# Expert biases as columns, an identity transposed at the head, indices in three operations, and a new plan for a two-layer kernel

## The chip, the cores and the metric

The kernel runs on one core of a Trainium2 chip. Its engines are TensorE (PE, matmuls), VectorE (DVE), ScalarE (ACT), GpSimd (POOL) and SyncE (SP, which here only issues transfers). The metric is the device time in microseconds (us) of one execution, as a median of several. A profiled execution gives a trace of every instruction; its times are counted from the start of its span.

## What is computed

Eight sequences (B = 8) of 512 positions and 256 features pass through two layers. The first is a feed-forward layer whose weights are chosen for each sequence from eight experts by an index. The second is an attention layer with 16 heads of 16 features, with a bias for every head and pair of positions and a mask, scaled and shifted by an embedding of a timestep, and a feed-forward layer behind it. Everything is fp32.

```python
h = gelu(x @ Wi[e] + bi[e]); o = h @ Wo[e] + bo[e]          # e = expert index of the sequence
x = layernorm(o + x) * gamma[e] + beta[e]
emb = silu(sin_emb(timestep)) @ W_ada + b_ada
x = layernorm(x) * (1 + scale) + shift                       # scale, shift from emb
q, k, v = x @ Wq + bq, x @ Wk + bk, x @ Wv + bv              # 16 heads
p = softmax(where(mask, -inf, q @ k.T / 4 + fside))
x = x + (p @ v) @ Wo + bo
x = x + gelu2(layernorm(x) * g2 + beta2) @ W1 ... @ W2 + b2  # 1024 hidden features
```

An index that is negative counts from the end and is then held within 0 to 7, as array indexing does.

## The kernel before

**A planner orders the work.** The kernel doesn't write its instructions in the order of its loops. Each piece of work is an operation (`op`) with an engine, a cost, a key, operations that it depends on, and buffers that it takes and uses. `Weave.run` then simulates the engines: at each turn it takes, for every engine, the operations that could start earliest, picks among those within 0.25 us the one of the lowest key (with an extra charge for another activation table or another way of tiling PE), and emits the one that starts first. Only operations with a key up to 14 above the lowest unfinished one are considered. The order of the program on each engine is that order; at run time the engines are held together by semaphores alone. The keys are in units of score steps.

**The work.** For every sequence b there are these groups:
- *Up*: 8 tiles of hidden features, each two accumulating 128x512 matmuls (`up`, line 687), and a Gelu on ScalarE (line 792) whose per-partition bias is a column of the tile `bc[b]`. Up needs the transposed input `xt` and the weights `wi[b]`.
- *Down*: 4 tiles of rows, each 8 accumulating 128x256 matmuls (line 710), and on VectorE an addition (line 805) and row statistics.
- *Norm*: two layer norms on GpSimd, ScalarE and VectorE.
- *Project* (line 861; transposes at line 665) and *values* (line 909): queries, keys and values.
- 16 *score steps*, of 32 query rows each for all heads, 128 in all. A step loads 1 MB of `fside` (line 1108), forms scores in four PSUM banks (lines 1138 and 1145), adds the bias and takes the row maximum on VectorE (line 1168), takes the exponential on ScalarE (line 1189) and transposes 32x32 blocks on VectorE (line 1204). In odd steps GpSimd adds the mask (line 1160). After every fourth step PE sums the values (line 1244) and multiplies by the output weights (line 1287).
- *last norm, last up, last down*: the second feed-forward layer, for the last sequence in three parts (line 1050). Its two hidden matmul groups use lines 687 and 710 as well.

An fp32 matmul is two pairs of a weight load and a matmul in the trace. All matmuls but the score and value sums use one of four PSUM buffers, `d`.

**The places.** `place` spreads the operations of a group evenly, by cost, from the first number of its entry in `PLACES` to the second; the third is how much lower the keys of its VectorE, ScalarE and GpSimd operations are. `DUE` and `LAST_DUE` give the keys of a step's operations relative to the step, `AHEAD` how far ahead of its first user a weight load is keyed, `PUT_BACK` the extra charges.

**The head.** The eight expert indices are loaded by a ScalarE DMA, turned into numbers within 0 to 7 by five VectorE operations on one row of eight (lines 391 to 397), and read by SyncE (line 431). Only then can SyncE issue the loads of the first expert's weights, the first `wi` in four pieces (line 474). GpSimd builds a 128x128 identity, `ident`.

**The expert bias** of 1024 numbers is loaded as 8 rows of 128 (line 462, `br`), transposed by PE against the identity (line 777), and copied to `bc` by VectorE (line 781). Another small transpose of this kind, for the shared biases, is at line 565.

**Instruction packets.** PE's instructions come from memory in packets of 256, by DMA. The planner counts PE's instructions (`words`), and takes it that the next packet is asked for at word 155 of each 256, and needed at word 192; it lands 2.4 us after it is seen by a queue. PE operations that would run past the last packet on hand are delayed in the plan. A load of 0.3 MB or more isn't started in the plan until `CLEAR` microseconds after a packet was asked for, and at run time such a load waits for the PE operation that ends behind that point (`behind`).

Of the kernel before, what the change touches and what calls it, by code (L numbers as in the profile page):

```python
# [16 lines left out]
ALU = mybir.AluOpType  # L17
AX = mybir.AxisListType

P = 128  # L20
# [10 lines left out]
def _constants():  # L31
# [13 lines left out]
    for i in range(TURN_PIECES):  # L45
# [14 lines left out]
        (-38.45, -36.16, 8.44), (-17.59, -11.52, -8.19), (7.71, 9.93, 7.56), (16.68, 26.05, 3.41),  # L60
        (37.04, 39.22, 1.41), (59.52, 58.14, 7.23), (76.02, 83.59, 6.09), (97.99, 99.88, 6.32),
    ],
    "down": [
        (-14.3, -13.78, 4.95), (-7.57, 12.25, 5.14), (10.35, 8.93, 1.84), (18.31, 19.88, 3.05),
        (44.73, 48.47, 6.47), (60.22, 65.93, -5.3), (73.23, 78.37, -3.77), (99.19, 102.84, 4.19),
    ],
    "norm": [
        (9.12, -14.45, 12.84), (42.79, 181.18, 28.12), (35.59, 134.32, 11.46),
        (2.52, 203.96, -36.01), (60.29, 31.67, 7.3), (7.93, 107.02, -50.91), (98.6, -8.09, 1.62),
        (119.85, -6.52, 12.88),  # L70
    ],
    "project": [
        (-12.18, -6.14, -12.38), (15.67, 19.49, 12.1), (24.45, 26.05, -2.29),
        (42.28, 58.66, 8.57), (55.4, 64.48, -4.5), (77, 88.71, 1.56), (87.84, 91.44, -7.27),
        (100.45, 117.32, -1.06),
    ],
    "values": [
        (3.18, -1.06, 7.82), (14.22, 38.5, 0.11), (40.15, 46.1, 4.42), (52.04, 62.66, 4.96),
        (64.28, 58.7, -11.65), (93.83, 89.56, 8.58), (110.2, 99.31, 6), (116.12, 120, 0.53),
    ],  # L80
    "last_norm": [
        (20.41, 6.88, -6.37), (35.57, 32.95, -7.85), (65.08, 42.97, -1.38), (80.61, 90.62, 2.89),
        (95.86, 82.62, 2.14), (101.58, 123.81, 3.25), (118.43, 130.96, -4.04),
    ],
    "last_up": [
        (28.71, 24.51, 4.43), (37.76, 39, -1.21), (60.99, 61.58, -1.11), (80.88, 87.68, 3.16),
        (102.11, 103.74, -0.13), (112.29, 122.71, -5.66), (126.48, 119.28, -4.58),
    ],
    "last_down": [
        (32.43, 20.21, -5.44), (59.59, 50.14, 4.98), (69.93, 70.07, 2.47), (87.34, 92.75, -0.01),  # L90
        (110.17, 115.86, 6.8), (124.14, 122.32, 5.45), (137.59, 134.49, -0.85),
    ],
    "last_part": [
        (131.42, 236.07, 2.43), (198.84, 229.52, -5.61), (222.05, 209.79, -2.84),
# [4 lines left out]
    "load_m": 2.79, "load_f": 2.99, "convert": 5.91, "add": 4.01, "neg": -0.08, "exp": 6.61,  # L99
    "turn": 9.37, "rec": 12.83, "diagonal": 7.66, "sums0": 5.09, "sums1": 6.11, "sums2": 12.85,  # L100
    "sums3": 7.94, "own": 7.57, "spread": 7.08, "divide": 7.96, "out": 9.83, "out_add": 12.81,
    "load_f2": 3.09, "masked": -0.48,
}
LAST_DUE = {
    "exp": 3.04, "turn": 11.23, "neg": 7.38, "rec": 14.33, "diagonal": 11, "sums0": 22.52,
    "sums1": 14.89, "sums2": 27.57, "sums3": 50.95, "own": 37.8, "spread": 42.01, "divide": 72.21,
    "out": 66.26, "out_add": 80.74,
# [3 lines left out]
    "table": 11.03, "tiles": 0.92,  # L111
# [3 lines left out]
    "xt": 6.18, "wi": 1.31, "br": 5.1, "x": 4.75, "wo": -1.82, "row": 23.23, "w1": -3.09,  # L115
    "w2": -0.62, "ss": 5.17, "bo": 18.56,
# [25 lines left out]
class Weave:  # L142
# [11 lines left out]
    CLEAR = 1.5  # L154

    def __init__(self):
        self.ops = []
# [21 lines left out]
    def run(self, behind):  # L179
# [11 lines left out]
        count, needed, asked, lands_at = 0.0, self.NEEDED, self.ASKED, [0.0]  # L191
        queue, clear, gate = 0.0, -100.0, None
        while left:
# [56 lines left out]
            if o.words:  # L250
                if count + o.words > needed:
                    needed += self.PACKET
                    lands_at.pop(0)
                if count + o.words > asked:
                    at = start + (asked - count) / o.words * o.cost
                    lands_at.append(max(at + self.SEEN, queue) + self.TAKES)
                    asked += self.PACKET
                    clear, gate = at + self.CLEAR, None
                count += o.words
# [25 lines left out]
def tile_expert_ffn_then_conditioned_layer(  # L285
# [46 lines left out]
    NJ = S // QB  # L332
    QS = 1.0 / math.sqrt(HD)
# [9 lines left out]
    def const(shape, name, dtype=F32):  # L343
        return pool.tile(shape, dtype, name=name)

    def slots(n, shape, name, dtype=F32):
        return Slots([pool.tile(shape, dtype, name=f"{name}_{i}") for i in range(n)])
# [16 lines left out]
    s_br = slots(2, [NF, P], "br")  # L364
# [26 lines left out]
    nc.vector.tensor_copy(idx_f, idx_in)  # L391
    idx_n = const([1, B], "idx_n")
    nc.vector.tensor_scalar(idx_n, idx_f, 0.0, float(E), ALU.is_lt, ALU.mult)
    nc.vector.tensor_tensor(idx_f, idx_f, idx_n, ALU.add)
    nc.vector.tensor_scalar(idx_f, idx_f, 0.0, float(E - 1), ALU.max, ALU.min)
    idx = const([1, B], "idx", I32)
    nc.vector.tensor_copy(idx, idx_f)
# [14 lines left out]

    def load(mb, key, emit, **kw):
        return op("SP", w.ISSUE, key, emit, mb=mb, **kw)

    xn, xt_h = [s_xn.new() for _ in range(B)], [s_xt.new() for _ in range(B)]
    br, bc = ([s.new() for _ in range(B)] for s in (s_br, s_bc))
# [11 lines left out]
    def at_expert(b):  # L429
        if b not in index:  # L430
            index[b] = nc.sync.value_load(idx[0:1, b : b + 1], min_val=0, max_val=E - 1)
        return bass.ds(index[b], 1)
# [8 lines left out]
    def load_first(b, mb, key, what, emit, **kw):  # L441
        return load_ahead(mb, what, emit, **kw) if b else load(mb, key, emit, **kw)

    ld_x, ld_xt, ld_wi, ld_wo, ld_bo_e, ld_rows, ld_br = {}, {}, {}, {}, {}, {}, {}
    for b in range(B):
# [15 lines left out]
        def br_in(b=b):  # L461
            nc.sync.dma_start(br[b].tile, e_bi[at_expert(b)].rearrange("o (c p) -> (o c) p", p=P))
# [20 lines left out]
        ld_br[b] = load_first(b, 0.02, -38.97, "br", br_in, takes=[br[b]])  # L483
# [286 lines left out]
    def expert_layer(b):  # L770
# [3 lines left out]
        h = s_d.new()  # L774
        a = op(
            "PE", 0.2, 0,
            lambda: nc.tensor.transpose(h.tile[:, :NF], br[b].tile, ident[:NF, :NF]),
            deps=[ld_br[b]], takes=[h], uses=[br[b]], words=2,
        )
        e = op(  # L780
            "DVE", 0.2, 0, lambda: nc.vector.tensor_copy(bc[b].tile, h.tile[:, :NF]),
            deps=[a], takes=[bc[b]], uses=[h],
        )
        turned = (0.2, [(a, 0.0), (e, -1.0)])
# [4 lines left out]
        def make(f, h, a):  # L789
            return op(  # L790
                "ACT", 0.7, 0,
                lambda: nc.scalar.activation(  # L792
                    hid.tile[:, f, :], h.tile, AF.Gelu, bias=bc[b].tile[:, f : f + 1]
                ),
                deps=[a, e], uses=[h, bc[b], hid], table="gelu",
            )

        hids = up(first, lambda: rising(wi[b]), (ld_wi[b], wi[b]), xt, [ld_xt[b]], hid, make)
        first.insert(3 if b == 0 else 0, turned)
# [295 lines left out]
    def attention_step(s):  # L1095
# [61 lines left out]
        if not joins:  # L1157
            for u in range(NU):
                def put_mask(u=u):
                    nc.gpsimd.tensor_tensor(f()[:, u, :], f()[:, u, :], mh.tile, ALU.add)  # L1160

                masked[u] = op(
                    "POOL", 1.25, s + due("masked", s), put_mask, deps=[lf, mc], uses=[pair, mh]
                )
# [182 lines left out]
def _laid_out(name, a):  # L1347
# [10 lines left out]
    elif name == "x":  # L1358
        b, s, d = a.shape
        a = a.reshape(b, s // P, P, d).transpose(0, 2, 1, 3)  # L1360
    elif name == "L0_cond_Wo":
# [48 lines left out]
```

## Time and profile before

| | |
|---|---|
| median of 3 runs | 908.43 us (904.48 to 909.48) |
| profiled execution | 906.64 us |
| its span, first to last instruction | 904.8 us |
| 128x512 matmuls of line 687 | 480 |
| 128x256 matmuls of line 710 | 1024 |
| score matmuls, line 1145 | 2048 |
| value sums, line 1244 | 8192 |
| first and last score step | at 73.3 and 858.5 us |
| bytes moved by DMA | 198.00 MB, 219 GB/s |
| GpSimd busy, ScalarE busy | 603.6 us, 687.1 us |

A row of the timeline gives the start, how long the row lasts, the engine (PEld is PE loading weights; a q behind a name is its queue), the line, the operation, the tile written and those read, the shape, how many instructions the row merges, and in brackets the idle time of the engine before it and what ended that. A row of the waits gives the engine, its line, what it waited for, and then microseconds in total, the number of waits, and the longest. "issue" is a wait for nothing that the profile shows, the arrival of instructions among it. The durations of matmuls include their way through the array, so they overlap; the spacing of their starts says how fast they follow each other.

### The profile page before, as it was taken

How to read it: one execution, taken by the hardware profiler on the slowest of the kernel's cores; microseconds unless marked ns; L12 is line 12 of the kernel's file. 1: busy time of each engine (PE TensorE's matmuls, PEld its weight loads, DVE VectorE, ACT ScalarE, POOL GpSimd, SP SyncE). 2: the span in 40 equal slices, each digit the busy share in tenths (PEclk: the TensorE clock that was granted, in tenths of full speed). 3: DMA queues.
4: the chain of work that ended last, by engine and by line, in shares of the span. 5: the costliest groups of instructions: out<-in, count | busy, mean ns of one | idle time of the engine just before them, and what ended most of it. 6: DMA issues, size and time to landing. Idle time of an engine off the chain costs nothing.

```text
span 904.8 us, 32061 instructions
## 1 busy us (share of the span) xinstructions
PE 884.0 (98%) x13329; PEld 522.7 (58%) x13329; DVE 737.5 (82%) x1715; ACT 687.1 (76%) x1522; POOL 603.6 (67%) x716
## 2 busy tenths in 40 slices
PE   7999999999989999999999999999999999999998
PEld 2664464654654655545657557466555555465687
DVE  1227999999978997999978999889789999999841
ACT  2347969869948977699784895998778977988743
POOL 1176887777779746767684976549786876685510
PEclk9999999999999999999999999999999999999999
DMA  6476555555575564666737667536745566665410
GB/s 237 165 299 267 224 215 230 214 204 227 214 313 217 200 245 168 221 254 241 280 136 276 235 245 293 211 133 265 288 163 219 205 242 241 248 242 221 172 60 24
DMA packets 43160, 198.00 MB, mean 219 GB/s; under 512 B 4772, under 2 KB 12278, under 8 KB 24582
## 3 DMA queue, kind: packets, MB, share of 16 engines
q1 hardware_dynamic: 42724, 195.91, 56.9%
q8 instruction: 104, 1.70, 0.8%
q14 instruction: 42, 0.34, 0.1%
q10 hardware_dynamic: 290, 0.04, 0.0%
HBM read 191.73 MB, written 4.21 MB: 217 GB/s over the span
## 4 chain that ended last, share of the span: by engine, by line
PE 87%; DMA 5%; ACT 3%; issue 2%; POOL 1%; DVE 1%; SPq 1%; DVEq 0%; POOLq 0%; ACTq 0%
PE d L710 23%; PE d L687 20%; PE d L1244 13%; PE sc L1145 12%; PE d L861 6%; DMA fs<-in_fside_Bx16xSxS_dram 3%; PE d L1287 3%; PE d L909 3%; PE sc L1138 2%; PE d L665 2%; PE d L1050 2%; ACT fs L1189 1%; POOL fs L1160 1%; PE d L1260 1%; DMA wo_t<-in_L_cond_Wo_dram 1%
## 5 line engine op out<-in xcount | busy, mean ns | idle before, releaser
L1189 ACT ACTIVATE fs<-fs,top 128x512 f32<-128x512 f32 x512 | 363.1, 712 | 62.1 <-POOL top L1181 61.6
L1168 DVE CUSTOM_DVE_ANT_0 fs<-sc,fs 128x512 f32<-128x512 f32 x512 | 325.2, 683 | 41.2 <-PE sc L1145 18.7
L1160 POOL TENSOR_TENSOR fs<-fs,mh 128x512 f32<-128x512 f32 x256 | 291.0, 1163 | 44.3 <-DMA fs<-in_fside_Bx16xSxS_dram 36.3
L1204 DVE STREAM_TRANSPOSE fs<-fs 128x1024 f32<-128x1024 f32 x256 | 304.9, 1219 | 4.9 <-ACT fs L1189 4.7
L710 PE MATMUL d<-w,hid 128*128 128x256 f32 x1024 | 239.7, 385 | 0.0
L687 PE MATMUL d<-xt,w 128*128 128x512 f32 x480 | 224.2, 607 | 8.1 <-DMA w<-in_L_cond_Wi_dram 6.7
L710 PEld LDWEIGHTS d<-w,hid 128*128 128x128 f32 x1024 | 189.1, 190 | 59.0 <-issue 31.1
L687 PEld LDWEIGHTS d<-xt,w 128*128 128x128 f32 x480 | 87.2, 191 | 123.2 <-issue 97.1
L1244 PEld LDWEIGHTS d<-fs,vb 64*32 64x32 f32 x8192 | 113.3, 105 | 48.1 <-issue 34.0
L1145 PE MATMUL sc<-k,q 32*64 32x512 f32 x2048 | 139.2, 600 | 0.0
L1244 PE MATMUL d<-fs,vb 64*32 64x128 f32 x8192 | 133.2, 272 | 2.4 <-issue 2.4
L1189 ACT ACTIVATION_READ_ACCUMULATOR fs<-fs,top 128x1 f32 x512 | 96.9, 189 | 0.0
L1120 POOL TENSOR_SCALAR mh<-m 128x512 bf16<-128x512 uint8 x128 | 79.7, 622 | 25.0 <-PE sc L1138 9.3
L1181 POOL TENSOR_SCALAR top<-top 128x4 f32<-128x4 f32 x128 | 25.4, 198 | 104.1 <-DVE top L1168 98.0
L792 ACT ACTIVATE hid<-d,bc 128x512 f32<-128x512 f32 x64 | 41.4, 686 | 29.1 <-PE d L687 19.9
L1145 PEld LDWEIGHTS sc<-k,q 32*64 32x64 f32 x2048 | 36.2, 130 | 32.9 <-issue 14.6
L728 DVE BATCH_NORM_STATS2 st<-xn 128x6 f32<-128x256 f32 x96 | 40.2, 419 | 15.5 <-POOL xn L762 13.3
L1189 ACT ACT_TABLE_LOAD x36 | 46.2, 1283 | 0.6
L1225 POOL TENSOR_TENSOR dg<-cst,den 128x512 f32<-128x512 f32 x32 | 34.1, 1066 | 17.1 <-DVE den L1220 14.5
L1168 DVE DVE_READ_ACCUMULATOR2_ANT top<- 128x1 f32 x512 | 42.5, 83 | 0.0
L984 ACT ACTIVATE hid<-d,col 128x512 f32<-128x512 f32 x56 | 35.9, 686 | 7.5 <-PE d L687 7.2
L762 POOL TENSOR_TENSOR xn<-xn,rows 128x1024 f32<-128x1024 f32 x16 | 37.9, 2371 | 4.8 <-ACT xn L741 4.0
(100 smaller groups left out, 753.3 us busy)
## 6 DMA issues: line engine op xcount, KB each, us to landing
fs<-in_fside_Bx16xSxS_dram SPq DMA_DIRECT2D x128, 1024.0 KB, 8.1
w<-in_L_cond_W_dram SPq DMA_DIRECT2D x16, 1024.0 KB, 6.4
w<-in_L_cond_Wo_dram SPq DMA_DIRECT2D x8, 1024.0 KB, 10.6
m<-in_mask_Bx1xSxS_bk_dram SPq DMA_DIRECT2D x32, 256.0 KB, 5.4
w<-in_L_cond_Wi_dram SPq DMA_DIRECT2D x7, 1024.0 KB, 6.0
xt<-in_x_turned_dram SPq DMA_DIRECT2D x8, 512.0 KB, 3.7
xn<-in_x_dram SPq DMA_DIRECT2D x8, 512.0 KB
out_dram<-xn SPq DMA_DIRECT2D x32, 128.0 KB, 3.4
```

The lines of the kernel that those rows point to most:

```text
L687: nc.tensor.matmul(h.tile, wt[:, c, f * P : (f + 1) * P], src.tile[:, c, :], start=(c == 0), stop=(c == ND - 1),)
L710: nc.tensor.matmul(h.tile[:, :D], lhs(f), wt[:, f, :], start=(f == 0), stop=(f == n - 1))
L728: nc.vector.bn_stats(st, src[:, t, :])
L792: lambda: nc.scalar.activation(hid.tile[:, f, :], h.tile, AF.Gelu, bias=bc[b].tile[:, f : f + 1]),
L861: nc.tensor.matmul(h.tile, wt[:, c, g * P : (g + 1) * P], x1t.tile[:, c, :], start=(c == 0), stop=(c == ND - 1),)
L1120: nc.gpsimd.tensor_scalar(mh.tile, m8.tile[:, s % NI, :].bitcast(U8), MASKED, 1.0, ALU.mult, ALU.mult)
L1145: nc.tensor.matmul(banks[u][64 * r : 64 * r + 64, :], q_h[b].tile[quads[u], r, i, :], k_h[b].tile[quads[u], r, :], start=not joins, stop=True,
L1160: nc.gpsimd.tensor_tensor(f()[:, u, :], f()[:, u, :], mh.tile, ALU.add)
L1168: nc.vector.tensor_tensor_reduce(out=f()[:, u, :], in0=banks[u], in1=f()[:, u, :], scale=1.0, scalar=-3.0e38, op0=ALU.add, op1=ALU.max, ac ...
L1189: nc.scalar.activation(f()[:, u, :], f()[:, u, :], AF.Exp, bias=top.tile[:, u : u + 1], accum_out=den.tile[:, u, s % NI : s % NI + 1],)
L1204: nc.vector.transpose(two, two)
L1244: nc.tensor.matmul(pc[r].tile[QB * u : QB * u + QB, :P], vb_h[b].tile[half, j, u, :], t[half, :, :, u, QB * j : QB * j + QB], start=(j == ...
```

## The change

- Indices: the cast to f32 is left out, the comparison and the addition read the int32 row, and the last operation writes int32. Three VectorE operations in place of five.
- Head: 18 transposes of the identity are issued on PE ahead of everything else, into a PSUM buffer that is not read. They need only `ident`. The planner's count of PE's instructions starts at 36.
- Expert biases: the input is laid out by the host as (expert, 128, 8), so that a DMA writes `bc[b]` directly, 8 numbers to each of 128 partitions. The transposes at line 777 and the copies at line 781 go, and the Gelus depend on the load itself.
- Planner: a packet is asked for no earlier than the one before it has landed, and `CLEAR` is 0.4 in place of 1.5. The cost of the mask addition is 1.17 in place of 1.25.
- All of `PLACES`, `DUE`, `LAST_DUE`, `PUT_BACK` and `AHEAD` have new numbers.

```diff
--- before.py
+++ after.py
@@ -57,63 +57,64 @@
 
 PLACES = {
     "up": [
-        (-38.45, -36.16, 8.44), (-17.59, -11.52, -8.19), (7.71, 9.93, 7.56), (16.68, 26.05, 3.41),
-        (37.04, 39.22, 1.41), (59.52, 58.14, 7.23), (76.02, 83.59, 6.09), (97.99, 99.88, 6.32),
+        (-35.52, -11.64, 4.94), (-11.9, -22.54, -2.99), (10.31, 12.14, 8.37),
+        (14.25, 22.85, -1.17), (36.77, 36.76, 1.07), (60, 57.83, 3.43), (73.83, 70.58, 4.85),
+        (94.92, 94.18, 8.26),
     ],
     "down": [
-        (-14.3, -13.78, 4.95), (-7.57, 12.25, 5.14), (10.35, 8.93, 1.84), (18.31, 19.88, 3.05),
-        (44.73, 48.47, 6.47), (60.22, 65.93, -5.3), (73.23, 78.37, -3.77), (99.19, 102.84, 4.19),
+        (-27.61, -24.87, -12.02), (-10.68, 13.31, -0.1), (15.13, 9.61, 0.32),
+        (18.1, 22.84, -6.64), (37.6, 44.8, 6.55), (61.84, 71.13, 6.87), (71.01, 75.76, -11.57),
+        (94.27, 108.04, 4.72),
     ],
     "norm": [
-        (9.12, -14.45, 12.84), (42.79, 181.18, 28.12), (35.59, 134.32, 11.46),
-        (2.52, 203.96, -36.01), (60.29, 31.67, 7.3), (7.93, 107.02, -50.91), (98.6, -8.09, 1.62),
-        (119.85, -6.52, 12.88),
+        (16.76, 0.43, 33.63), (50.75, 236.12, 35.78), (19.13, 112.89, 1.36),
+        (-0.73, 150.66, -35.12), (51.98, -3.26, 10.27), (19.84, 116.2, -46.57),
+        (91.19, 25.08, -4.73), (110.17, -11.25, 3.62),
     ],
     "project": [
-        (-12.18, -6.14, -12.38), (15.67, 19.49, 12.1), (24.45, 26.05, -2.29),
-        (42.28, 58.66, 8.57), (55.4, 64.48, -4.5), (77, 88.71, 1.56), (87.84, 91.44, -7.27),
-        (100.45, 117.32, -1.06),
+        (-3.93, 2.03, -2.64), (13.32, 15.26, 2.77), (19.23, 30.34, -1.82), (36.97, 59.93, 8.33),
+        (59.15, 43.96, -0.28), (76.77, 86.46, -0.67), (94.5, 91.24, 3.27), (102.9, 113.31, 0.58),
     ],
     "values": [
-        (3.18, -1.06, 7.82), (14.22, 38.5, 0.11), (40.15, 46.1, 4.42), (52.04, 62.66, 4.96),
-        (64.28, 58.7, -11.65), (93.83, 89.56, 8.58), (110.2, 99.31, 6), (116.12, 120, 0.53),
+        (7.77, 10.24, 3.39), (15.24, 37.1, -8.26), (43.61, 43.86, 7.08), (45.49, 67.83, -2.21),
+        (67.46, 56.65, -3.66), (87.64, 97.81, 9.29), (105.15, 97.2, 1.98), (117.06, 118.69, 4.47),
     ],
     "last_norm": [
-        (20.41, 6.88, -6.37), (35.57, 32.95, -7.85), (65.08, 42.97, -1.38), (80.61, 90.62, 2.89),
-        (95.86, 82.62, 2.14), (101.58, 123.81, 3.25), (118.43, 130.96, -4.04),
+        (18.93, 10.43, -5.55), (50.08, 53.52, 3.27), (67.69, 61.42, 9.62), (72.79, 86.37, -9.45),
+        (92.08, 89.98, -0.52), (115.23, 113.98, 8.28), (117.57, 113.58, -3.53),
     ],
     "last_up": [
-        (28.71, 24.51, 4.43), (37.76, 39, -1.21), (60.99, 61.58, -1.11), (80.88, 87.68, 3.16),
-        (102.11, 103.74, -0.13), (112.29, 122.71, -5.66), (126.48, 119.28, -4.58),
+        (26.27, 38.03, 1.01), (46.54, 47.77, 0.5), (64.51, 62.2, 1.22), (85.68, 84.44, 5.39),
+        (107.94, 99.87, -3.13), (108.88, 120.89, 3.43), (128.3, 135.79, 3.82),
     ],
     "last_down": [
-        (32.43, 20.21, -5.44), (59.59, 50.14, 4.98), (69.93, 70.07, 2.47), (87.34, 92.75, -0.01),
-        (110.17, 115.86, 6.8), (124.14, 122.32, 5.45), (137.59, 134.49, -0.85),
+        (35.14, 24.23, -5.08), (61.9, 51.71, 11.65), (77.75, 75.33, -0.48), (91.52, 78.58, 2.9),
+        (102.76, 117.32, 4.72), (116.43, 125.64, -1.72), (134.83, 134.55, 3.99),
     ],
     "last_part": [
-        (131.42, 236.07, 2.43), (198.84, 229.52, -5.61), (222.05, 209.79, -2.84),
+        (132.72, 239.72, 0.26), (186.35, 240.12, 6.14), (193.91, 245.56, -3.6),
     ],
 }
 
 DUE = {
-    "load_m": 2.79, "load_f": 2.99, "convert": 5.91, "add": 4.01, "neg": -0.08, "exp": 6.61,
-    "turn": 9.37, "rec": 12.83, "diagonal": 7.66, "sums0": 5.09, "sums1": 6.11, "sums2": 12.85,
-    "sums3": 7.94, "own": 7.57, "spread": 7.08, "divide": 7.96, "out": 9.83, "out_add": 12.81,
-    "load_f2": 3.09, "masked": -0.48,
+    "load_m": -10.02, "load_f": -1.89, "convert": 7.1, "add": 3.28, "neg": -0.39, "exp": 5.75,
+    "turn": 9.93, "rec": 13.65, "diagonal": 9.39, "sums0": 8.89, "sums1": 5.6, "sums2": 10.17,
+    "sums3": 6.54, "own": 5.17, "spread": 6.3, "divide": 6, "out": 5.97, "out_add": 12.92,
+    "load_f2": -1.22, "masked": 0.86,
 }
 LAST_DUE = {
-    "exp": 3.04, "turn": 11.23, "neg": 7.38, "rec": 14.33, "diagonal": 11, "sums0": 22.52,
-    "sums1": 14.89, "sums2": 27.57, "sums3": 50.95, "own": 37.8, "spread": 42.01, "divide": 72.21,
-    "out": 66.26, "out_add": 80.74,
+    "exp": 5.76, "turn": 8.18, "neg": 13.36, "rec": 10.03, "diagonal": 19.1, "sums0": 23.45,
+    "sums1": 25.82, "sums2": 41.29, "sums3": 33.28, "own": 38.66, "spread": 31.04,
+    "divide": 34.93, "out": 67.43, "out_add": 77.99,
 }
 
 PUT_BACK = {
-    "table": 11.03, "tiles": 0.92,
+    "table": 7.19, "tiles": 0.72,
 }
 
 AHEAD = {
-    "xt": 6.18, "wi": 1.31, "br": 5.1, "x": 4.75, "wo": -1.82, "row": 23.23, "w1": -3.09,
-    "w2": -0.62, "ss": 5.17, "bo": 18.56,
+    "xt": 1.02, "wi": 3.02, "br": 19.67, "x": -1.86, "wo": 2.29, "row": 24.21, "w1": 7.1,
+    "w2": 8.89, "ss": -2.85, "bo": 20.55,
 }
 
 
@@ -151,10 +152,10 @@
     CHANGE = {"dense": 0.2, "scores": 0.1, "sums": 0.14}
     PACKET, ASKED, NEEDED, SEEN, TAKES = 256.0, 155.0, 192.0, 1.0, 2.4
     ISSUE, BEGINS, RATE, LANDS, LARGE, NEAR, HOLD = 0.45, 1.2, 0.37, 0.8, 0.3, 100.0, 4.0
-    CLEAR = 1.5
+    CLEAR = 0.4
 
     def __init__(self):
-        self.ops = []
+        self.ops, self.sent = [], 0.0
 
     def op(self, engine, cost, key, emit, deps=(), takes=(), uses=(), table=None, mb=0.0,
            words=0, tiles="dense"):
@@ -188,8 +189,8 @@
                 open_ops[o.engine].append(o)
         by_key = sorted(self.ops, key=lambda o: o.key)
         lowest, table, tiles, left = 0, None, None, len(self.ops)
-        count, needed, asked, lands_at = 0.0, self.NEEDED, self.ASKED, [0.0]
-        queue, clear, gate = 0.0, -100.0, None
+        count, needed, asked, lands_at = self.sent, self.NEEDED, self.ASKED, [0.0]
+        queue, clear, gate, landed = 0.0, -100.0, None, 0.0
         while left:
             while by_key[lowest].done:
                 lowest += 1
@@ -252,8 +253,9 @@
                     needed += self.PACKET
                     lands_at.pop(0)
                 if count + o.words > asked:
-                    at = start + (asked - count) / o.words * o.cost
-                    lands_at.append(max(at + self.SEEN, queue) + self.TAKES)
+                    at = max(start + (asked - count) / o.words * o.cost, landed)
+                    landed = max(at + self.SEEN, queue) + self.TAKES
+                    lands_at.append(landed)
                     asked += self.PACKET
                     clear, gate = at + self.CLEAR, None
                 count += o.words
@@ -330,6 +332,7 @@
     NU = 4
     NI = P // QB
     NJ = S // QB
+    WARM = 18
     QS = 1.0 / math.sqrt(HD)
 
     pool = ctx.enter_context(tc.tile_pool(name="sb", bufs=1))
@@ -361,7 +364,6 @@
     s_w = slots(2, [P, NF * D], "w")
     s_bo = slots(2, [P, D], "bo")
     s_rows = slots(2, [P, 2, D], "rows")
-    s_br = slots(2, [NF, P], "br")
     s_bc = slots(2, [P, NF], "bc")
     s_xt = slots(2, [P, ND, S], "xt")
     s_q = slots(2, [P, ND, NQ, 2 * QB], "q")
@@ -388,13 +390,10 @@
     ident = const([P, P], "ident")
     make_identity(nc, ident)
     idx_f = const([1, B], "idx_f")
-    nc.vector.tensor_copy(idx_f, idx_in)
-    idx_n = const([1, B], "idx_n")
-    nc.vector.tensor_scalar(idx_n, idx_f, 0.0, float(E), ALU.is_lt, ALU.mult)
-    nc.vector.tensor_tensor(idx_f, idx_f, idx_n, ALU.add)
-    nc.vector.tensor_scalar(idx_f, idx_f, 0.0, float(E - 1), ALU.max, ALU.min)
+    nc.vector.tensor_scalar(idx_f, idx_in, 0.0, float(E), ALU.is_lt, ALU.mult)
+    nc.vector.tensor_tensor(idx_f, idx_in, idx_f, ALU.add)
     idx = const([1, B], "idx", I32)
-    nc.vector.tensor_copy(idx, idx_f)
+    nc.vector.tensor_scalar(idx, idx_f, 0.0, float(E - 1), ALU.max, ALU.min)
     half_power = const([P, NT], "half_power")
     nc.gpsimd.memset(half_power, -0.5)
     small = const([P, 2, NT], "small")
@@ -410,11 +409,17 @@
         return row.unsqueeze(1).to_broadcast([P, NT, D])
 
 
+    warm = s_d.free[-1][1]
+    for _ in range(WARM):
+        nc.tensor.transpose(warm[:, :P], ident, ident)
+    w.sent = 2.0 * WARM
+
+
     def load(mb, key, emit, **kw):
         return op("SP", w.ISSUE, key, emit, mb=mb, **kw)
 
     xn, xt_h = [s_xn.new() for _ in range(B)], [s_xt.new() for _ in range(B)]
-    br, bc = ([s.new() for _ in range(B)] for s in (s_br, s_bc))
+    bc = [s_bc.new() for _ in range(B)]
     e_bo_h, rows = ([s.new() for _ in range(B)] for s in (s_bo, s_rows))
     wi, wo_e, w1_h, w2_h = ([s_w.new() for _ in range(B)] for _ in range(4))
 
@@ -459,7 +464,7 @@
             nc.sync.dma_start(wo_e[b].tile, e_wo[at_expert(b)].rearrange("o p n -> p (o n)"))
 
         def br_in(b=b):
-            nc.sync.dma_start(br[b].tile, e_bi[at_expert(b)].rearrange("o (c p) -> (o c) p", p=P))
+            nc.sync.dma_start(bc[b].tile, e_bi[at_expert(b)].rearrange("o p c -> p (o c)"))
 
         ld_xt[b] = load_first(b, 0.5, -40, "xt", xt_in, takes=[xt_h[b]])
         if b:
@@ -480,7 +485,7 @@
                     0.25, -39 + 0.01 * n, piece_in, deps=[known], uses=[wi[b]]
                 )
                 ld_wi[b] += [o, o]
-        ld_br[b] = load_first(b, 0.02, -38.97, "br", br_in, takes=[br[b]])
+        ld_br[b] = load_first(b, 0.02, -38.97, "br", br_in, takes=[bc[b]])
         ld_x[b] = load_first(b, 0.5, -37.5, "x", x_in, takes=[xn[b]])
         ld_wo[b] = load_first(b, 1.0, -37, "wo", wo_in, takes=[wo_e[b]])
         def bo_in(b=b):
@@ -771,17 +776,6 @@
 
         first, second, third = [], [], []
         xt, hid = xt_h[b], s_hid.new()
-        h = s_d.new()
-        a = op(
-            "PE", 0.2, 0,
-            lambda: nc.tensor.transpose(h.tile[:, :NF], br[b].tile, ident[:NF, :NF]),
-            deps=[ld_br[b]], takes=[h], uses=[br[b]], words=2,
-        )
-        e = op(
-            "DVE", 0.2, 0, lambda: nc.vector.tensor_copy(bc[b].tile, h.tile[:, :NF]),
-            deps=[a], takes=[bc[b]], uses=[h],
-        )
-        turned = (0.2, [(a, 0.0), (e, -1.0)])
         bias = pool_rows(
             first, b, [ld_x[b], ld_bo_e[b]], lambda: e_bo_h[b].tile, ALU.add, [e_bo_h[b]]
         )
@@ -792,11 +786,10 @@
                 lambda: nc.scalar.activation(
                     hid.tile[:, f, :], h.tile, AF.Gelu, bias=bc[b].tile[:, f : f + 1]
                 ),
-                deps=[a, e], uses=[h, bc[b], hid], table="gelu",
+                deps=[a, ld_br[b]], uses=[h, bc[b], hid], table="gelu",
             )
 
         hids = up(first, lambda: rising(wi[b]), (ld_wi[b], wi[b]), xt, [ld_xt[b]], hid, make)
-        first.insert(3 if b == 0 else 0, turned)
         mv = s_mv.new()
         sums = []
         for t in range(NT):
@@ -1160,7 +1153,7 @@
                     nc.gpsimd.tensor_tensor(f()[:, u, :], f()[:, u, :], mh.tile, ALU.add)
 
                 masked[u] = op(
-                    "POOL", 1.25, s + due("masked", s), put_mask, deps=[lf, mc], uses=[pair, mh]
+                    "POOL", 1.17, s + due("masked", s), put_mask, deps=[lf, mc], uses=[pair, mh]
                 )
         adds = []
         for u in range(NU):
@@ -1358,6 +1351,9 @@
     elif name == "x":
         b, s, d = a.shape
         a = a.reshape(b, s // P, P, d).transpose(0, 2, 1, 3)
+    elif name == "L0_cond_bi":
+        e, f = a.shape
+        a = a.reshape(e, f // P, P).transpose(0, 2, 1)
     elif name == "L0_cond_Wo":
         e, f, d = a.shape
         a = a.reshape(e, f // P, P, d).transpose(0, 2, 1, 3).reshape(e, P, f // P * d)
```

## The prediction

> **What bounds the kernel now.** I read the page's busy times first, then what TensorE waited for, then the head and two places of the timeline.
>
> ```profile
> PE 884.0 (98%) x13329; PEld 522.7 (58%) x13329; DVE 737.5 (82%) x1715; ACT 687.1 (76%) x1522; POOL 603.6 (67%) x716
> ```
>
> TensorE (PE) is busy for 884.0 of 904.8 us. Its matmul ends are modelled, so I checked by start-to-start spacing: 128x512 matmuls follow each other every 0.43 us and 128x256 ones every 0.216 us almost everywhere. PE is the bound. Only its idle time, its half-speed time and its own removable instructions can be won; VectorE's 82% matters only where it could take over. The waits view, PE alone, says where PE idles (us in total, times, longest):
>
> ```profile
> PE d L687 <- DMA w<-in_L_cond_Wi_dram: 6.7, 1, 6.7
> PE d L1244 <- issue: 2.4, 3, 1.4
> PE d L1287 <- DVE ctx L1277: 1.9, 1, 1.9
> PE d L687 <- ACT hid L792: 1.2, 2, 0.6
> PE d L777 <- DMA br<-in_L_cond_bi_dram: 1.2, 1, 1.2
> PE d L665 <- issue: 0.9, 1, 0.9
> PE d L1050 <- issue: 0.6, 1, 0.6
> ```
>
> So 6.7 us pass before the first matmul, 1.2 us wait for one bias DMA, about 4 us are waits on data, and the "issue" rows (2.4 + 0.9 + 0.6, and three smaller ones of 1.0 together) make 4.9 us. After the last matmul, at 901.2, 3.6 us are output. The head, in the timeline's weight-load rows (start, duration):
>
> ```profile
> 7.69 0.33 PEld L687 LDWEIGHTS d<-xt,w 128*128 128x128 f32 x1 [0.52 <-issue]
> 8.54 0.33 PEld L687 LDWEIGHTS d<-xt,w 128*128 128x128 f32 x1 [0.52 <-issue]
> 9.39 0.33 PEld L687 LDWEIGHTS d<-xt,w 128*128 128x128 f32 x1 [0.52 <-issue]
> 10.04 0.19 PEld L687 LDWEIGHTS d<-xt,w 128*128 128x128 f32 x1 [0.31 <-issue]
> 10.47 0.19 PEld L687 LDWEIGHTS d<-xt,w 128*128 128x128 f32 x1 [0.24 <-issue]
> ```
>
> Until 9.39 the spacing is 0.85 us, from 10.04 on 0.43. The 0.65 between them is a change of speed at about 9.8: PE works at half speed for its first 3.1 us.
>
> **The change, part by part**, summed against the profiled execution: 906.64 us, a span of 904.8 and 1.8 around it. That is 1.8 below the median of the runs, 908.43; I apply the difference to the median.
>
> Indices. The five VectorE operations on the index row start at 1.93, 2.12, 2.32, 2.51 and 2.70, so one costs 0.19. SyncE reads the index at 2.89, issues the first Wi piece at 3.88, and PE starts at 6.70 when it lands. Nothing else is late: x-turned was issued at 0.73. Two operations less is 0.38 earlier. A comparison reading int32 instead of f32 is taken at the same price (the int32 cast costs 0.16 like the rest); bounds 0.2 to 0.4. **-0.4.**
>
> Warm-up. The first eight matmuls run from 6.70 to 11.76, 5.06 us; at 0.43 each and 0.1 for the start they take 3.54. Full speed from the start is worth 1.5. The price of the 18 transposes: eight of line 665 take 1.09 us with 0.27 modelled drain, so 0.117 each, 0.234 at half speed, 4.2 in all. The identity is ready at 1.30; they run from 1.4 to 5.6 at latest, before the first Wi piece lands at 6.3, so nothing queues behind them. If 3.1 us of work release the clock, that is at 4.5, they end at about 5.1, and 1.2 us of idle time follow. [...] I take the row's end, **-1.5**, bounds 0 and -1.5; a loss needs the transposes to outlast 6.3.
>
> Bias columns. Eight transposes on PE (L777) and eight copies on VectorE go. From 78.96 to 81.04 a group of eight matmuls of line 710 with one L777 behind it takes 2.08; the same group alone (76.10 to 77.92) takes 1.82. So 0.26 each: 0.25 for b=0 and 1.6 for b=2 to 7. For b=1:
>
> ```profile
> 19.84 2.74 PE L687 MATMUL d<-xt,w 128*128 128x512 f32 x6
> 23.80 0.19 PE L777 MATMUL d<-ident,br 8*128 8x8 f32 x1 [1.23 <-DMA br<-in_L_cond_bi_dram]
> 24.14 0.21 PE L565 MATMUL d<-ident,br_t 18*128 18x18 f32 x1
> 24.27 1.99 PE L710 MATMUL d<-w,hid 128*128 128x256 f32 x8
> ```
>
> PE's stream ends at 22.41, L777 waits until 23.80 for a bias issued only at 21.68, and the down matmuls start at 24.27. Take L777 away and the next-late thing is their own input: the last Gelu runs from 22.61 to 23.30, so they start at about 23.4, 0.85 earlier; bounds 0 (if the new order puts something as late there) and 1.85 (if another matmul group fills the hole). Together **-2.7**. The new bias transfer has 128 pieces of 32 bytes in place of 8 of 512; SyncE's issue stays at 0.34, and the timestep transfer on the ScalarE queue is the same shape and size. Now the Gelu waits for it directly. In the head it is issued at about 4.7 and wanted at 8.0; if late, PE has four PSUM buffers, 6.9 us of work, before it notices. Zero, with the later ones issued ahead; 1 us at worst, once.
>
> The order. All places, due times and issue leads change, so every queue is reshuffled: SyncE's weight, mask and fside loads, GpSimd's mask work and the orders on PE, VectorE and ScalarE. The old trace cannot show this order. What it shows is why two of the planner's constants change:
>
> ```profile
> 287.23 2.00 PE L1244 MATMUL d<-fs,vb 64*32 64x128 f32 x124
> 290.65 0.30 PE L1244 MATMUL d<-fs,vb 64*32 64x128 f32 x2 [1.42 <-issue]
> ```
>
> PE stops for 1.42 us in mid-group with no wait in the profile. From 283 to 289 the 16 DMA engines carry nothing but two instruction packets of PE, begun at 283.81 and 287.79, each taking over 1.4 us: the second is asked for late, not held up by data. The old planner let a packet be under way while the last hadn't landed; the new one asks after it, so it sees such stalls and can order around them. [...] The rows decide that there is something to win, but a planner that sees a stall needn't avoid it. I take **-1.5** of the 4.9, bounds -4.9 and +3. The shorter hold of large loads behind a packet (1.5 to 0.4) starts held loads up to 1.1 us earlier; PE waits on data about 4 us in all, and a new order makes its own such waits: 0, bounds -2 and +4.
>
> Sum: -0.4 - 1.5 - 2.7 - 1.5 = -6.1. Profiled execution 900.5; median **902.3**.
>
> **Rivals.** *Only the removed instructions count*: the clock is not released before the data come and the new order stalls on fetch as before. -0.4 - 2.7 = -3.1: 905.3. [...] Against: the 3.1 us release.
>
> *The new order also empties PE's idle places*: 0.4 + 1.5 + 2.7 + 4.9, 1.0 more from the hole at 22.41 and 2 of the data waits, 12.5 in all: 895.9. Against it: the stalls have three different causes (fetch, DMA, VectorE), and all would have to go at once.
>
> *Slower: score steps run out of filler.* Each score step needs VectorE for four adds at 0.61 and two transposes at 1.22, 4.9 us; PE's idle is avoided by dense matmuls put between steps. Spreading each dense line evenly over its places, the old tables put 65 us of dense work between steps 16 and 28 (the Up and Down of b=3, Project of 1 and 2, most of last Up and Down of 0), the new ones 40: Project of 1 falls before, last Up of 0 behind. These twelve steps took from 166 to 237, 71 us. With 25.1 less PE needs 46.1, VectorE 12 x 4.9 = 58.8. If PE keeps strictly to the places it idles 12.7 us there, and the result is 908.4 - 4.6 + 12.7 = 916.5 (the fetch gain counted out). It makes the kernel measurably slower once the idle time passes 4.6 + 4.5, so when the planner pulls less than 3.6 us of later work forward. Against it:
>
> ```profile
> 84.18 3.70 PE L687 MATMUL d<-xt,w 128*128 128x512 f32 x8
> 87.81 1.11 PE L1145 MATMUL sc<-k,q 32*64 32x512 f32 x16
> 88.85 3.70 PE L687 MATMUL d<-xt,w 128*128 128x512 f32 x8
> ```
>
> This is Up of b=2, placed at 7.71 to 9.93, already running after step 2 (83.2): the planner fills PE with later work when a step isn't ready.
>
> **Chances.** The forecast 0.47 (its own range 899 to 904.5); only the removed instructions, or a new order that eats about that much, 0.25 (904 to 909); the emptied idle places 0.14 (895 to 899); slower 0.14 (913 to 925). A measurement here tells 0.5%, 4.5 us, from no change, so faster means below 903.9: 0.42 + 0.14 = 0.56. Within: 0.25 + 0.05 = 0.30. Slower: 0.14. The range 896.5 to 909.5 leaves out the slower case and part of the best.
>
> **What would show it.** Indices: the first L687 matmul at about 6.3. Warm-up: its weight loads at 0.19 from the first on, and the granted clock at full before 6.3. Bias: no row of L777, and the first L710 matmul at 24.27 - 0.4 - 1.5 - 0.25 - 0.85 = 21.3. Order: PE's "issue" rows at about 3.4 in all, and its waits on data still near 4. I am wrong if those waits exceed 8 us, if PE idles between steps 16 and 28 with VectorE near 100%, or if half-speed loads follow the transposes.

## The result, and the profile after

The changed kernel takes 915.97 us (median of 4 runs, 913.68 to 917.40) against 907.19 for the kernel before, measured beside it: 1.0094 times as long, 95% interval 1.0072 to 1.0117. It is 8.8 us slower, where 6.1 less was forecast. Its profiled execution took 913.68 us, with a span of 911.9. It is the fastest of the four.

The page's busy times and PE's waits in the changed kernel (us in total, times, longest; line 692 is line 687 before, 715 is 710, 1237 is 1244, 670 is 665, 1280 is 1287):

```profile
PE 887.1 (97%) x13339; PEld 526.1 (58%) x13339; DVE 734.9 (81%) x1705; ACT 699.6 (77%) x1530; POOL 601.9 (66%) x716
```

```profile
PE d L1237 <- issue: 4.6, 3, 2.8
PE d L692 <- ACT xt L965: 3.2, 2, 2.6
PE d L1237 <- ACT hid L977: 2.2, 1, 2.2
PE d L670 <- POOL xn L767: 1.9, 3, 1.0
PE d L1280 <- DVE ctx L1270: 1.6, 2, 1.4
PE d L715 <- DMA w<-in_L_cond_Wo_dram: 1.6, 1, 1.6
PE d L692 <- ACT hid L977: 1.3, 2, 1.1
PE d L692 <- DMA w<-in_L_cond_Wi_dram: 0.9, 1, 0.9
...
PE d L715 <- issue: 0.5, 1, 0.5
```

PE is still the bound and still nearly full. But the waits on other engines and on loads inside the kernel, without the head's two (1.4 for the identity and the 0.9 for Wi), add up to 14.0 us (11.8 in the rows shown), where before they were 5.1, the bias wait included. The issue rows stand at 5.1, against 4.9. They are called packet stalls below: in the traces of the two kernels their pauses of over 0.5 us, seven in all, each end 1.39 to 1.46 us after a packet of PE's instructions has landed.

The head, in weight-load rows of the changed kernel:

```profile
6.33 0.30 PEld L692 LDWEIGHTS d<-xt,w 128*128 128x128 f32 x2 [1.28 <-issue]
6.87 0.19 PEld L692 LDWEIGHTS d<-xt,w 128*128 128x128 f32 x1 [0.24 <-issue]
7.30 0.19 PEld L692 LDWEIGHTS d<-xt,w 128*128 128x128 f32 x1 [0.24 <-issue]
```

The first expert matmul starts at 6.36 instead of 6.70, and the loads are at full speed from there on, 0.43 us apart. No row of the bias transposes is left. The down matmuls start at 22.08 instead of 24.27, and the four condition matmuls, 1.8 us of PE, that before came at 33.10 now run ahead of them at 20.26. So PE is 4 us ahead at that point. All of it and 7.1 us of span more are lost behind.

Two places show how. Busy times by stretch in the changed kernel (start and end, length, then PE, PEld, DVE, ACT and POOL, the granted PE clock, the DMA share, GB/s):

```profile
320.00:323.50 3.50, 3.48 (x160) 2.84 (x152) 2.51 (x7) 3.19 (x8) 3.33 (x3) 1.00 0.03 7
323.50:326.00 2.50, 0.00 (x0) 0.00 (x0) 1.35 (x5) 2.50 (x10) 2.50 (x3) 1.00 0.49 157
326.00:330.00 4.00, 3.89 (x6) 1.80 (x7) 3.93 (x10) 2.24 (x6) 3.59 (x7) 0.57 0.99 412
```

PE has nothing to do for 2.6 us: the layer norm's transposes are issued, but ScalarE copies them out of PSUM (line 965) only after four exponentials and another copy, from 325.29 on. And the wait costs more than its length: behind it the granted clock is 0.57 over 4 us, which is half speed for 3.4 us; the four matmuls at 326.11 take 3.34 us instead of 1.72, another 1.6. Two of the other three executions had more of this: the mean granted clocks of the three are 0.996, 0.994 and 0.998, so by this estimate (one minus the clock, times the time) half clock cost them up to 3.7, 5.5 and 1.8 us. In 58 executions of the kernel before the mean clock was 0.998 twice and 0.999 or 1.000 in all others. The second place, in the timeline:

```profile
783.47 1.79 PE L1237 MATMUL d<-fs,vb 64*32 64x128 f32 x110
788.05 0.59 PE L1237 MATMUL d<-fs,vb 64*32 64x128 f32 x18 [2.78 <-issue]
```

This is a packet stall of the old kind, longer than any before (1.42). The new packet rule did not order around it.

### The profile page after: what moved, and what is told of

It is laid out like the page before. It is cut to its first block, busy times and chain, and to the rows that moved or that the text cites. A ratio compares the mean times of both kernels' runs of the same rounds, so it can differ in the third digit from the quotient of the medians.

```text
span 911.9 us, 32142 instructions
## 1 busy us (share of the span) xinstructions
PE 887.1 (97%) x13339; PEld 526.1 (58%) x13339; DVE 734.9 (81%) x1705; ACT 699.6 (77%) x1530; POOL 601.9 (66%) x716
## 4 chain that ended last, share of the span: by engine, by line
PE 68%; POOL 9%; ACT 7%; DMA 4%; issue 3%; DVE 2%; POOLq 0%; ACTq 0%; DVEq 0%; SPq 0%
PE d L715 18%; PE d L692 14%; PE d L1237 11%; PE sc L1138 10%; PE d L854 5%; POOL fs L1153 4%; ACT fs L1182 3%; DMA fs<-in_fside_Bx16xSxS_dram 3%; PE d L902 2%; POOL xn L767 2%; PE d L1280 2%; PE sc L1131 2%; PE d L1043 1%; PE d L670 1%; ACT xn L746 1%
## 5 line engine op out<-in xcount | busy, mean ns | idle before, releaser
L767 POOL TENSOR_TENSOR xn<-xn,bo 128x1024 f32<-128x1024 f32 x8 | 18.9, 2365 | 37.7 <-DMA xn<-in_x_dram 23.8
```

## The experiments

Theory 1: the edits of the program pay what was forecast, and the new order loses it. Theory 2: an edit costs the time. Theory 3: the shorter hold lets large loads get ahead of PE's packets. To separate them, the order must be kept: the planner re-deals every queue as soon as one cost or operation changes. So in the first kernels the planner still plans the old operations, L777 and L781 among them, with the old tables, but those two emit nothing, and the edits are made in what is emitted.

**f_all: the order before, the three edits.** The main lines:

```diff
-    lambda: nc.tensor.transpose(h.tile[:, :NF], br[b].tile, ident[:NF, :NF]),
+    lambda: None,
-    lambda: nc.vector.tensor_copy(bc[b].tile, h.tile[:, :NF]),
+    lambda: None,
-    nc.sync.dma_start(br[b].tile, e_bi[at_expert(b)].rearrange("o (c p) -> (o c) p", p=P))
+    nc.sync.dma_start(e_bc[:, b, :], e_bi[at_expert(b)].rearrange("o p c -> p (o c)"))
+    for _ in range(18):
+        nc.tensor.transpose(warm[:, :P], ident, ident)
     # and the three index operations of the change
```

The tile `e_bc` holds the columns of all eight sequences, and the host lays the biases out as in the change.

> The order of the kernel before on every engine, with only the three edits of the program made in it: three index operations, 18 identity transposes at the head, bias columns by DMA without PE's transposes and VectorE's copies. Theory 1 (the edits pay what was forecast, the new order loses it): 4.6 us less than before, about 902.6. Theory 2 (one of the edits costs what was lost, the small bias pieces or the Gelu waiting for their DMA): no gain, 907 or more.

Measured: 908.80 us beside 905.48 for before, 1.0032 (1.0020 to 1.0044). Slower, as Theory 2 has it. The next two kernels say which edit.

**f_bias: the bias columns alone.** The edit is the first six lines above.

> The order before, with the bias columns alone. Theory 1: 2.7 us less than before, about 904.5, the first down matmul at about 23.4. Theory 2: 907 or more, ScalarE waiting for the bias transfer ahead of its Gelus.

Measured: 902.21, ratio 0.9954 (0.9941 to 0.9967), 3.3 us less. The first down matmul starts at 23.06. Theory 1 for this edit; the small pieces cost nothing that shows.

**f_idx_warm: three index operations and 18 transposes alone.** The edit is the last three lines above.

> The order before, with the three index operations and the 18 identity transposes alone. Theory 1: 1.9 us less than before, about 905.3, the first expert matmul at about 6.3 at full clock. Theory 2 says nothing against it.

Measured: 920.48, ratio 1.0177 (1.0139 to 1.0216): 15 us slower, which neither theory had. The page shows the head as expected in its start, so the loss lies behind it. Waits of PE in this kernel, and one place of its timeline:

```profile
PE d L1246 <- issue: 9.5, 6, 4.2
PE d L1262 <- issue: 2.3, 3, 1.4
...
PE d L712 <- issue: 1.3, 1, 1.3
...
PE sc L1147 <- issue: 0.9, 3, 0.4
```

```profile
636.82 2.90 PE L1246 MATMUL d<-fs,vb 64*32 64x128 f32 x191
643.92 0.27 PE L1246 MATMUL d<-fs,vb 64*32 64x128 f32 x1 [4.20 <-issue]
```

PE waits 14.0 us for instructions, 9 more than before, and stands still for 4.2 us one matmul before the end of a group; the granted clock behind that is at half for 3.4 us (0.96 on average from 641 to 645, 0.62 from 645 to 649). This made Theory 4: 18 transposes are 36 instructions; they move every boundary of PE's packets of 256 by 36 against an order laid out around the old boundaries. The changed kernel tells its planner of them (`sent`); this kernel doesn't.

**f_all_hold04: f_all with the shorter hold at run time, order kept.** The main lines:

```diff
-    CLEAR = 1.5
+    CLEAR, GATE = 1.5, 0.4
-    clear, gate = at + self.CLEAR, None
+    clear, gate_at, gate = at + self.CLEAR, at + self.GATE, None
-    if o.words and clear > 0.0 and (gate is None or gate[0] < clear):
+    if o.words and clear > 0.0 and (gate is None or gate[0] < gate_at):
```

> As f_all, same order on every engine, but a large load waits at run time only for the PE operation that ends 0.4 us (not 1.5) after a packet of instructions was asked for. Theory 1 (order): within 1.5 us of f_all. Theory 3 (the shorter hold lets large loads get ahead of PE's instruction packets): at least 4 us more than f_all, with more of PE's waits on issue than the 4.9 us before.

Measured: 903.62, ratio 0.9975 (0.9962 to 0.9987): 5.2 us less than f_all. Theory 3 is refuted in this order; the shorter hold is a gain. This kernel issues what the changed kernel issues, 13,339 matmuls on PE in both, with the same 18 transposes and the same hold; only the order differs, and its planner doesn't count the 36 instructions. It takes 1.9 us less than the kernel before, the changed kernel 8.8 more: 10.6 us between the two orders (in ratios 0.9975 against 1.0094).

**f_two and f_two_hold04: the same warm-up length with 8 instructions.** Two fp32 matmuls of 512 columns keep PE busy for 3.8 us, as the 18 transposes do for 4.1.

```diff
-    for _ in range(18):
-        nc.tensor.transpose(warm[:, :P], ident, ident)
+    for _ in range(2):
+        nc.tensor.matmul(
+            warm, ident, ident.unsqueeze(1).to_broadcast([P, 4, P]), start=True, stop=True
+        )
```

> As f_all (order before, three edits), but TensorE is warmed by two 128x512 matmuls of the identity, 8 instructions, in place of 18 transposes, 36 instructions. The earlier run with the transposes and indices alone lost 15 us, with PE's waits on issue at 14 us. Theory 4 (the 36 instructions shift where PE's instruction packets of 256 end against the order, which the planner had not counted): with 8 the shift is small and the three edits pay: 4.6 us less than before, 901. Theory 5 (the warm-up or the index edit itself costs): 907 or more, as f_all.

> As f_two with the run-time hold of large loads at 0.4 us. f_all gained 5 us from it. If the shorter hold is a gain by itself (loads start earlier, PE waits less for data): 3 to 5 us less than f_two, about 897. If it was luck of that order: within 1.5 us of f_two.

Measured, beside 905.77 for before: f_two 899.35, ratio 0.9931 (0.9914 to 0.9947), 6.4 us less; f_two_hold04 896.96, ratio 0.9908 (0.9891 to 0.9926), 8.8 us less. Theory 4 holds: the same three edits lose 3.3 us with 36 instructions at the head and gain 6.4 with 8. The gain is more than 4.6 because f_two also meets fewer packet stalls: its issue waits are 0.8 in all, 4.1 less than before. That is luck of the boundaries, not the edits' own. The two intervals overlap, so the hold's gain is shown by the f_all pair, and here only by the rows of GpSimd's waits on `fside` loads, f_two and then f_two_hold04:

```profile
POOL fs L1165 <- DMA fs<-in_fside_Bx16xSxS_dram: 42.6, 23, 4.0
```

```profile
POOL fs L1166 <- DMA fs<-in_fside_Bx16xSxS_dram: 24.6, 18, 4.2
```

Loads that may start earlier keep GpSimd waiting 18 us less. f_two_hold04 is the best kernel of the study, faster than both. What is left of PE's waits in it, first rows and the packet row:

```profile
PE sc L1144 <- DVE top L1174: 1.8, 5, 0.6
PE d L571 <- DMA br_t<-in_L_cond_bv_dram: 1.7, 1, 1.7
PE d L1266 <- POOL dg L1231: 1.4, 1, 1.4
...
PE d L1250 <- issue: 0.6, 2, 0.5
```

**a_nowarm: the changed kernel's order without the 18 transposes that its planner counts.**

```diff
-    for _ in range(WARM):
-        nc.tensor.transpose(warm[:, :P], ident, ident)
```

> The changed kernel in its own order, without emitting the 18 transposes that its planner counts. Theory 4 (packet phase): slower than the changed kernel by more than the 1.5 us of the cold clock, 5 us or more, with more issue waits on PE. Theory 5 (the transposes cost): faster than the changed kernel.

Measured: 930.43, 14.5 us more than the changed kernel's 915.97. Theory 4 from the other side: take the 36 instructions away where the order counts on them, and the packet stalls go from 5.1 to 13.7 us. The rest goes with the cold clock at the head, 1.5 us by the weight-load rows of the kernel before, and with half clock: by the mean granted clocks of the profiled executions, 0.992 against 0.998, an estimated 5.6 us more. Its largest issue row:

```profile
PE d L1235 <- issue: 11.3, 8, 3.3
```

**a_hold15: the changed kernel's order with the old hold.** `CLEAR, GATE = 0.4, 1.5`, the other lines as in f_all_hold04.

> The changed kernel in its own order, large loads held at run time for 1.5 us behind the asking for a packet instead of 0.4. If the shorter hold is what lost the time (theory 3): 4 us or more less than the changed kernel. If the shorter hold is a gain by itself: 3 to 5 us more. If the order alone decides: within 1.5 us of the changed kernel.

Measured: 917.92 (912.14 to 922.95), within its spread of the changed kernel; the fastest of its four executions had a mean clock of 1.000, the slowest 0.990. The short hold did not lose the time here either; that it gains is not shown in this order.

So neither the edits nor the hold lost it, and f_all_hold04 beside the changed kernel shows that the order did. The tables, the packet rule and the mask's cost make that order together; no run takes them apart. The last four ask whether the planner saw the loss coming. By its own reckoning PE's work ends at 894.7 in the kernel before and at 897.4 in the changed one. **a_search1 and a_search2** are the changed kernel with tables found by changing one to three numbers at random and keeping what ended earlier. Nearly every number of the tables differs in each; two places of a_search1:

```diff
     "up": [
-        (-35.52, -11.64, 4.94), (-11.9, -22.54, -2.99), (10.31, 12.14, 8.37),
+        (-31.63, -15.05, 11.82), (-10.99, -21.06, -0.36), (10.84, 10.06, 7.85),
...
-    "table": 7.19, "tiles": 0.72,
+    "table": 7.88, "tiles": 0.65,
```

> The changed kernel with other places, found by trying numbers until the planner's own end of PE's work fell from 897.4 (the changed kernel; 894.7 for the kernel before) to 893.9; the order up to about 313 is that of the changed kernel. Its plan no longer has the 2.3 us hole at 322 that the chip showed as 2.6 us of idle PE and 3.4 us of half clock. Theory 6 (what the planner foresees is what is lost): 3.5 to 5 us less than the changed kernel, about 911 to 912.5. Theory 7 (waits that the planner doesn't see decide, and change with every order): anywhere from 903 to 925, and apart from the second search by more than 3 us.

> A second search of the same kind, with the planner's end at 894.2. Theory 6: within 1.5 us of the first search, about 912. Theory 7: apart from it by more than 3 us.

**s_oldplaces_newrule** is the changed program with the tables before. **b_jit0** is the kernel before with one number changed:

```diff
-    "table": 11.03, "tiles": 0.92,
+    "table": 11.03, "tiles": 0.90,
```

> The changed program and the new packet rule, planned with the old places, due times and charges; the planner ends at 940.8. Theory 6: about 43 us above the changed kernel, 955 to 960. If the old places are good and the new ones bad: about 900.

> The kernel before with one number changed by 2%: the charge for another tiling of PE is 0.90 in place of 0.92. The planner ends at 935.6 instead of 894.7. Theory 6: about 41 us above the kernel before, 945. If such a number does nothing on the chip: 906.

Measured, beside 907.14 for before (one execution each of the last two kernels):

| kernel | planner's end of PE | measured |
|---|---|---|
| before | 894.7 | 907.1 |
| changed | 897.4 | 916.0 |
| a_search1 | 893.9 | 912.5 (906.5 to 919.8) |
| a_search2 | 894.2 | 918.1 (916.1 to 919.5) |
| s_oldplaces_newrule | 940.8 | 952.2 |
| b_jit0 | 935.6 | 960.5 |

Coarsely the planner is right (Theory 6): the two orders that it puts 41 and 43 us later are 53 and 36 us slower, half clock included, which the planner doesn't count (mean clocks 0.980 and 0.986, so up to about 19 and 13 us of it). Tables fit one program only; a change of 2% in one number, or the changed program with the new packet rule, re-deals the queues, so the old tables could not just have been kept. Finer than that it doesn't tell orders apart (Theory 7): the first four rows lie within 3.5 us in the plan and 11 us apart on the chip, in another order. The two searched orders differ by 0.4 in the plan and by 5.6 on the chip (ratios 1.0025 to 1.0098 and 1.0097 to 1.0153, which just touch), and both stay slower than the kernel before, though planned to end earlier. Between their profiled executions, 6.0 us apart, packet stalls grow from 5.5 to 10.4 us, though the planner allows for packets, and the mean granted clock falls from 0.998 to 0.994, by the same estimate 1.8 and 5.5 us of half clock. In a_search2:

```profile
PE d L1318 <- issue: 9.4, 6, 3.1
```

## Why the prediction was wrong, point by point

**What bounds the kernel** was right: PE at 97%, and what was lost was lost as waits of PE and as half clock behind them.

**Indices, -0.4**: right. The three operations start at 1.93, 2.12 and 2.31, the first matmul comes 0.34 earlier.

**Warm-up, -1.5**: right in this profile, but not a fixed gain. Its bound of 0, which no row of the kernel before shows, was met too. The same 18 transposes left the clock at half speed in f_all:

```profile
9.02 0.34 PEld L690 LDWEIGHTS d<-xt,w 128*128 128x128 f32 x1 [0.52 <-issue]
9.87 0.34 PEld L690 LDWEIGHTS d<-xt,w 128*128 128x128 f32 x1 [0.52 <-issue]
10.53 0.19 PEld L690 LDWEIGHTS d<-xt,w 128*128 128x128 f32 x1 [0.32 <-issue]
```

That puts the change of speed near 10.3. In f_all_hold04 and f_two_hold04, warmed as well, it was over by 7: PE has six matmuls between 7 and 9 in both, and three in f_all. f_two's weight loads still took 0.33 at 8.21. The stretches between changes of the clock are whole multiples of 3.413 us (last section), and a grid of such windows, counted back from the release, fits what happened. In the kernel before the window from 6.41 to 9.83 has PE busy for 3.13 us, and the clock is released at its end. In the changed kernel the window from 2.12 to 5.53 is filled by the transposes (PE busy for 3.33 us of it) and the clock is released at its end; in f_all they fall into two windows, PE busy for 2.12 and 2.54 us, and neither releases it. By this grid it was where a window began that made the difference, with the same transposes. And 1.5 is not all kept: in f_two_hold04, warmed, PE then waits 1.7 us for `br_t`, and the down matmuls start at 22.14; in f_two, cold, at 22.28. The prediction named the last Gelu as next-late in that hole; in the old order it is this load. The new order filled the hole instead.

**What the edit of the warm-up costs** was priced at nothing beside the time that PE spends on it. That step failed as a statement about the edit: 36 instructions that the planner doesn't count move the packet boundaries, and what this costs depends on where they come to lie: 15.0 us in f_idx_warm, 6.6 in f_all against f_bias, 14.5 in a_nowarm with its clock losses. The changed kernel's planner counts the 36, and its packet stalls are about as before, 5.1 us against 4.9, so this is not what slowed it.

**Bias columns, -2.7**: 3.3 measured in f_bias, where some of it is fewer packet stalls (2.2 in place of 4.9) and new waits take part back.

**The order** is the step that failed: "a new order makes its own such waits: 0, bounds -2 and +4", and "-1.5 of the 4.9" for the packet stalls. Measured, waits on other engines and loads went from 5.1 to 14.0, +8.9, past the bound and past the 8 us that the prediction had named as its sign of being wrong; packet stalls went from 4.9 to 5.1 instead of down; and half clock behind one of the waits added 1.6, for which the sum had no term. With the gains that did come (0.34 at the start, 1.5 of clock at the head, 8 x 0.26 of transposes) that makes +6.8, of the 7.1 us by which the span grew. Against f_all_hold04, the same instructions in the old order, whose span is 902.5, the changed kernel is 9.4 us longer: 7.6 more of waits on engines and loads (14.0 against 6.4), 1.6 more of packet stalls (5.1 against 3.5) and 1.6 of half clock, in sum 1.4 too much, which these rows don't explain. The bounds came from the size of the old waits. But the old waits were those of one order that had come out well, the best of the six in the table, which lie between 907 and 960. Six orders, not drawn alike, show that orders differ by far more than 4 us; that an order dealt anew should be expected to be worse is an argument from them, not a measurement.

**The slower rival** had the number, 916.5 against 915.97, by luck: its mechanism was wrong. Steps 16 to 28 run from 168 to 241.8 in the changed kernel, with PE busy for 73.2 of 73.8 us. PE did not run out of work there.

What stays open is why the planner, which allows for packets and for busy engines, misses some stalls by 2 to 3 us, and with it why this order came out so. The count of PE's instructions is not it: the planner counts 26,780 for the changed kernel, the trace has 26,789 (13,339 matmuls, as many weight loads, and 111 others).

## What to carry to other kernels

When an order is laid out by a planner, treat a change of its tables as a new order, and ask how far the times of such orders lie apart, not how large the present waits are. To learn what an edit is worth, keep the order and emit the edit into it. Count what an edit adds to the instruction stream of an engine that runs close to its packets: two long matmuls kept PE busy for 3.8 us and eighteen transposes for 4.1, with 8 instructions against 36, and f_two took 899.35 us, f_all 908.80.

## What the runs showed of the hardware

- PE's 26,789 instructions in the changed kernel came with 104 transfers of 16 KB on one DMA queue, one for about 256 instructions. After a stall for instructions PE goes on about 1.4 us after the packet's own transfer ends (566.57 to 568.03, and 786.66 to 788.05, in the changed kernel). The traces of the kernel before and the changed kernel have seven pauses of over 0.5 us for instructions, and this lag is 1.39 to 1.46 us in every one. No two of the packets begin closer than 3.34 us in the first trace and 3.33 in the second, though the value sums use up 256 instructions in about 2 us (117 matmuls with their weight loads in 1.94 us, at 564.59).
- In the changed kernel PE idle for 2.6 us was followed by 3.4 us of half clock at 326; idle for 2.8 at 785 was not. The records of the granted clock fit one reason: in both traces the stretches between its changes, after the first release, are whole multiples of 3.413 us (262 of them in the kernel before; 94, 1 and 171 in the changed one). On this grid the shorter pause falls into one window, and PE is busy for 0.78 us of it; the longer one falls across two, and they keep 1.50 and 2.54:

```profile
322.97:326.38 3.41, 0.78 (x6) 0.55 (x5) 1.70 (x7) 3.41 (x10) 3.41 (x3) 1.00 0.47 163
326.38:329.79 3.41, 3.41 (x5) 1.38 (x5) 3.38 (x8) 1.86 (x5) 3.09 (x6) 0.50 1.01 416
783.77:787.18 3.41, 1.50 (x109) 1.23 (x87) 3.28 (x6) 3.41 (x11) 1.06 (x1) 1.00 0.78 322
787.18:790.59 3.41, 2.54 (x101) 1.49 (x105) 0.71 (x3) 2.30 (x4) 0.62 (x1) 1.00 0.27 50
```

- After the first release two windows of this grid left PE idle for over three quarters of their length within the two spans: 77% from 322.97 to 326.38 in the changed kernel, 87% from 900.71 to 904.12 in the kernel before. Half clock followed both. The next in idle time, 56% from 783.77, 49% from 718.92 and 47% from 432.20 in the changed kernel, were followed by full clock. Where between 56 and 77% the change lies is open, and so is what brought the mean clock of b_jit0 down to 0.980.
